# Condensing channel statistics as the last measuring step, and exchanging which engine copies which convolution outcome, in the first layer of a four-layer network

## The chip, the core and the metric

The kernel runs on one core of one Trainium2 chip. A core has a matrix engine (TensorE, "PE" in the profile; its weight loads are listed apart as "PEld"), VectorE ("DVE"), ScalarE ("ACT"), GpSimd ("POOL") and SyncE ("SP"), which issues most of the DMA. Every engine works through its own list of instructions in order and waits for the others by semaphores. The metric is the device time of one execution in microseconds (us), lower is better; the time of a kernel is the median of its runs.

## What is computed

The input is a batch of 8 images of 56x56 pixels with 192 channels, float32. Four layers follow each other, each of the form `x = x + layer(groupnorm(x))`. The change lies in layer 0 and in the statistics that layer 0 leaves for layer 1. Cut to what matters:

```python
def _gn(v, G=32, eps=1e-5):          # 32 groups of 6 channels, per image
    g = v.reshape(B, H, W, 32, 6)
    m, s = g.mean((1, 2, 4)), g.var((1, 2, 4))
    return (g - m) / sqrt(s + eps)

def layer0(x):                       # x: normalized, 8 x 56 x 56 x 192
    p, q, v = silu(x @ Wp + bp), silu(x @ Wq + bq), silu(x @ Wv + bv)   # 576 channels each
    qv = q * v
    o1 = toeplitz(qv along width, a1)    # per channel, a 56x56 Toeplitz matrix
    o2 = toeplitz(qv along height, a2)
    return (p * (o1 + o2)) @ Wo + bo
x = x + layer0(_gn(x)); x = x + layer1(_gn(x)); x = x + layer2(_gn(x)); x = x + layer3(_gn(x))
```

## The kernel before

**Tiling.** Layer 0 takes one image `b` after another. The 576 channels of `q*v` are cut into 9 subchunks of 64 channels; they are worked on in five blocks `c` = 0 to 4 of two subchunks each (the last block has one). A block consists of these steps:

- `project`: for each of four groups of pixel rows, `gate` multiplies by the weights (12 matmuls, line 356) and ScalarE takes silu of the result into a buffer `s` (L364); `products` then multiplies q by v: `straight` on VectorE (L378), `across` on GpSimd and partly on VectorE (L384). All of them write the tile `qv`.
- `turn_both` (or `turn` in the last block): seven (four) steps in which TensorE transposes a part of `qv` into PSUM (L411, L430); VectorE copies one half of it out (tile `ol`) and after it ScalarE the other (tile `or`), L416 and L437.
- `convolve`: for each of its subchunks two steps q = 0 and 1 of 32 matmuls (L454). Each step fills one PSUM tile, its "outcome", which one engine copies into the tile `ot`: VectorE for q = 0 (L474), ScalarE for q = 1 (L472). A block has so four such steps, and four copies, one after the other. In the last block (`tail`) the two engines share each copy in another way (L465), which the change leaves alone.
- After the blocks 1 and 3, `post` works off a pair of blocks: `gate` (12 matmuls a part, L496, silu in L503), `back` (transposes of `ot`, L515, and a multiplication, L520), `out` and `rest` (L529, L550) with sums into the image's result `acca`, `accb` (L481, L483). `post_tail` does so after block 4.

**PSUM.** `banks()` hands out PSUM tiles in a ring: three tiles named `c`, and every fourth time one named `o` (in the blocks 2 and 4 the `o` tile is used by `out`, and `banks()` gives `c` alone while the steps of `post` run). A matmul that wants a tile waits until the copies out of its last content are done. The buffers `s` are a ring of six.

**Statistics.** `gn.steps` returns for a set of spans a list of measuring steps (`measure`, one `bn_stats` each, L156), and two more functions. `deviate` condenses the measured statistics with one `bn_aggr` for each span (L160), copies the means into one tile (L161), and hands them to `spread`, which multiplies them by a small matrix on TensorE (L129) and copies the result back (L137, L138); then come three small VectorE operations (L163, L164, L165). `settle` spreads the deviations (L129 again), takes the root on ScalarE (L170) and forms scale and bias (L171, L172). There are two users:

- `normalize(nxt)`, the next image's input, measured in block 2 (12 measuring steps);
- `tell(b - 1, ...)`, the finished image's result, for layer 1 (11 measuring steps: six in block 0, the other five in block 1). Its `deviate` and `last` are the list `telling`. For the last image, `tell` is called after the loop: its steps run at the end of layer 0, and its `telling` goes to `cx.late`, which layer 1 calls.

**Order.** The order of the instructions of TensorE, VectorE and ScalarE is the program's own (`manual_schedule`). In block 1 it is

```python
merge(weave(fill, [f for fs, _ in early for f in fs]), turns, measures)
for _, f in early: f()                      # products of the groups 0 and 1
...
beside = [lambda f=f: f(banks) for f in telling]
ahead = whole(ahead, beside)                # groups 2 and 3: gates, one of beside, products
```

`weave` spreads several lists evenly over one another, so that the seven turns, the gates of the first groups and the measuring steps alternate. `whole` puts `deviate` between the gates of group 2 and its products, and `last` between the gates of group 3 and its products. After that come the four convolution steps. In block 3 the products of the last group stand in front of the first convolution step, and `post` follows the fourth. The transfers on SyncE and GpSimd's work are put in order by a scheduler.

Of the kernel before, what the change touches and what calls it, by code (L numbers as in the profile page):

```python
# [99 lines left out]
class GroupNormSplit:  # L100
# [40 lines left out]
    def steps(self, *spans):  # L141

        cx, nc = self.cx, self.cx.nc
        c = len(spans)
        new = lambda name: cx.tile(self.small, [128, c], f"{name}{c}")
        mv = cx.tile(self.small, [128, c, 2], f"mv{c}")
        mean, dev, told = new("mean"), new("dev"), {}
        parts = [  # L150
            (x, n, cx.tile(self.small, [128, n, 6], f"st{c}{k}")) for k, (x, n) in enumerate(spans)
        ]

        def measure(x, n, st, j):
            w = x.shape[-1] // n
            nc.vector.bn_stats(st[:, j, :], x[:, j * w : (j + 1) * w])  # L156

        def deviate(bank):
            for k, (_, _, st) in enumerate(parts):
                nc.vector.bn_aggr(mv[:, k, :], st.rearrange("p a b -> p (a b)"))  # L160
            nc.vector.tensor_copy(mean, mv[:, :, 0])  # L161
            told["gms"] = gms = self.spread(bank, mean)
            nc.vector.tensor_tensor(dev, mean, gms, ALU.subtract)  # L163
            nc.vector.tensor_tensor(dev, dev, dev, ALU.mult)  # L164
            nc.vector.tensor_tensor(dev, dev, mv[:, :, 1], ALU.add)  # L165

        def settle(bank):
            sd, rstd, nbias = new("sd"), new("rstd"), new("nbias")
            gms = told["gms"]
            nc.scalar.activation(sd, self.spread(bank, dev), AF.Sqrt, bias=self.eps)  # L170
            nc.vector.reciprocal(rstd, sd)  # L171
            nc.vector.scalar_tensor_tensor(nbias, gms, -1.0, rstd, ALU.mult, ALU.mult)  # L172
            return rstd, nbias

        return [lambda p=p, j=j: measure(*p, j) for p in parts for j in range(p[1])], deviate, settle


def layer0(cx, xin, xout, w, consts):
# [6 lines left out]
    tc, nc = cx.tc, cx.nc  # L185
# [8 lines left out]
    with ExitStack() as es:  # L194
# [9 lines left out]
        def banks():  # L204
            if ring["wide"]:
                ring["at"] += 1
                if ring["at"] % 4 == 0:
                    return cx.tile(psc, [128, 2, 512], "o", bufs=1)
            return cx.tile(psc, [128, 2, 512], "c")
# [231 lines left out]
        def convolve(n, ot):  # L441


            s = n % NS
            left, right = pairs[n % 2]
            tail = s == NS - 1

            def step(q):
                ps = banks()
                for k in range(2):  # L450
                    for v in range(8):
                        for u in range(2):
                            d = q * 16 + 8 * k + v + u * 32
                            nc.tensor.matmul(  # L454
                                ps[u * 64 : (u + 1) * 64, k, v * H : (v + 1) * H],
                                left[:, d * H : d * H + 64],
                                right[:, d * H : (d + 1) * H],
                                start=True, stop=True, skip_group_check=True,
                            )
                if tail:  # L460
                    for u, copy in enumerate((nc.vector.tensor_copy, nc.scalar.copy)):
                        d0 = q * 16 + u * 32
                        dst = ot[0:H, :, d0 : d0 + 16].rearrange("p h (k v) -> p h k v", k=2)
                        src = ps[u * 64 : u * 64 + H, :, 0 : 8 * H]
                        copy(dst, src.rearrange("p k (v h) -> p h k v", h=H))  # L465
                    return
                else:
                    d0 = s % 4 * 32 + 16 * q
                    dst = ot[:, :, d0 : d0 + 16].rearrange("p h (k v) -> p h k v", k=2)
                    src = ps[0:120, :, 0 : 8 * H].rearrange("p k (v h) -> p h k v", h=H)  # L470
                if q % 2:
                    nc.scalar.copy(dst, src)  # L472
                else:
                    nc.vector.tensor_copy(dst, src)  # L474

            return [lambda q=q: step(q) for q in range(2)]

        def add(m, j, x, ps):
# [114 lines left out]
        def post_tail(xn, ot, acc):  # L593
# [67 lines left out]

            steps = [lambda f=f, g=g: f(g) for f in (gate, back, out) for g in range(2)]
            return [*steps, lambda: (rest(0), rest(1))]

        def ready(v):
# [3 lines left out]
        def normalize(xn):  # L669

            measures, deviate, settle = gn.steps(*((xn[:, k], 4) for k in range(3)))

            def last():
                rstd, nbias = settle(banks)
                ready(rstd)
                for k in (0, 2):
                    affine(nc.vector, xn[:, k], xn[:, k], rstd[:, k : k + 1], nbias[:, k : k + 1])
                nc.scalar.activation(
                    xn[:, 1], xn[:, 1], AF.Identity, bias=nbias[:, 1:2], scale=rstd[:, 1:2]
                )  # L680

            return measures, [lambda: deviate(banks), last]

        def tell(b, xa, xb):

            measures, deviate, settle = gn.steps((xa, 7), (xb, 4))

            def last(bank):
                nn = cx.tile(gn.small, [128, 2, 2], "nn")
                told = settle(bank)  # L690
                if b + 1 < B:
                    ready(told[0])
                for i, v in enumerate(told):
                    nc.vector.tensor_copy(nn[:, :, i], v)
                nc.sync.dma_start(cx.norms[b][0:CA], nn[:, 0, :])
                nc.sync.dma_start(cx.norms[b][CA:], nn[0:CB, 1, :])

            return measures, [deviate, last]
# [25 lines left out]
        def whole(steps, beside=()):  # L724

            k, n = len(beside), max(len(steps), 1)
            cuts = [beside[-(-i * k // n) : -(-(i + 1) * k // n)] for i in range(n)]
            return [
                lambda fs=fs, h=h, cut=cut: [f() for f in (*fs, *cut, h)]
                for (fs, h), cut in zip(steps, cuts)  # L730
            ]

        merge(whole(project(xn, 0)))
        fill, after, telling, measures = [], None, [], []
        for b in range(B):
            more = b + 1 < B
            for c in range(NC):
# [9 lines left out]
                if c == 2 and more:  # L747
                    measures, normalizing = normalize(nxt)
                merge(weave(fill, [f for fs, _ in early for f in fs]), turns, measures)
                measures = []  # L750
# [8 lines left out]
                if c == 0:  # L759
                    if after is not None:  # L760
                        image_dma(nc.sync, xout[b - 1], *after, store=True)
                        measures, telling = tell(b - 1, *after)
                        beside, measures = measures[:6], measures[6:]
# [1475 lines left out]
```

## Time and profile before

The kernel's median was 4032.93 us in 3 runs (4031.6 to 4044.12). The profiled execution took 4030.25 us by itself, 2.68 us less than the median; its span from the first to the last instruction is 4028.5 us, so 1.75 us lie around it.

| stretch of the profiled execution | us | TensorE busy | VectorE busy | ScalarE busy | GpSimd busy |
|---|---|---|---|---|---|
| whole span | 4028.5 | 3786.9 | 2382.0 | 1792.8 | 1511.3 |
| 640 to 880, a piece of layer 0 | 240 | 229.25 | 149.77 | 107.18 | 75.27 |
| 880 to 1120, a piece of layer 0 | 240 | 229.43 | 153.35 | 110.30 | 75.43 |
| 2160 to 4028, the layers after | 1868 | 1782.96 | 1089.68 | 874.30 | 837.36 |

Layer 0 ends shortly after 1890 us. One image takes about 229 us there: the stretch in which the means of the finished image are spread starts at 578.96, 807.98, 1036.21 and so on.

How to read the lines further down. A line of the waits reads: engine, tile and line that waited, what it waited for, the time in total, how often, the longest. A line of the timeline has the start, the duration (of the whole group when several are merged, xcount), engine, line, operation, output and input with shapes, and in brackets the idle time of that engine just before and what ended it. A line of the windows has the stretch, its length, the busy time, then the clock that TensorE was granted (1.00 is full speed), the share of the DMA engines and GB/s.

### The profile page before, as it was taken

Reading aid. Unit: us, or ns where it says so; the run is one execution under the profiler, and the core shown is the slowest. Engines: PE = TensorE matmul, PEld = TensorE weight load, DVE = VectorE, ACT = ScalarE, POOL = GpSimd, SP = SyncE. Lnnn points to the kernel's source line nnn. Section 1 sums busy time; section 2 is a strip of 40 time slices with the busy share of each in tenths; the row PEclk is TensorE's granted clock in tenths of the full one; section 3 lists DMA queues with packets and bytes.
Section 4 is the critical chain, followed back from the end, with each engine's and each line's share of the span. In section 5 each row is a group of like instructions: output and inputs, shape, how many; then the busy total and the mean of one; then the engine's idle time right before and its main releaser. Section 6 shows DMA issues by size and latency. Waiting matters only on the chain.

```text
span 4028.5 us, 115826 instructions
## 1 busy us (share of the span) xinstructions
PE 3786.9 (94%) x51036; PEld 2655.0 (66%) x51036; DVE 2382.0 (59%) x3270; ACT 1792.8 (45%) x2036; POOL 1511.3 (38%) x1325
## 2 busy tenths in 40 slices
PE   6989999999999999998899999899989999998997
PEld 4777767777777767776566666444445455556997
DVE  5647666665656666556444444666666667665664
ACT  2444444443444444343343343244345555554663
POOL 3222242323232242223333333333334444444776
PEclk9999999999999999999899999999999999999999
DMA  7865262434426253333344443556557766653333
GB/s 158 168 139 146 78 169 78 129 85 111 103 82 165 78 141 94 88 93 106 77 109 104 113 95 96 173 174 198 176 162 187 178 147 153 152 139 102 99 101 99
DMA packets 390300, 507.94 MB, mean 126 GB/s; under 512 B 176932, under 2 KB 326724, under 8 KB 388404
## 3 DMA queue, kind: packets, MB, share of 16 engines
q1 hardware_dynamic: 385621, 494.07, 47.3%
q8 instruction: 401, 6.57, 0.7%
q10 hardware_dynamic: 3135, 3.47, 0.3%
q0 software_dynamic: 1040, 2.99, 0.3%
q14 instruction: 103, 0.84, 0.1%
HBM read 344.69 MB, written 155.65 MB: 124 GB/s over the span
## 4 chain that ended last, share of the span: by engine, by line
PE 73%; DVE 9%; issue 6%; DMA 4%; ACT 3%; POOL 2%; SPq 1%; DVEq 0%; POOLq 0%; ACTq 0%
PE c L356 9%; PE h L2072 8%; PE v L1560 6%; PE c L496 5%; PE c L454 4%; PE o L529 4%; PE c L1079 4%; PE o L356 3%; PE y L1114 3%; PE kv L1620 3%; PE c L550 2%; PE c L1085 2%; DVE qv L378 2%; PE c L1782 2%; DVE ol L416 2%
## 5 line engine op out<-in xcount | busy, mean ns | idle before, releaser
L384 POOL TENSOR_TENSOR qv<-s,s 128x392 f32<-128x392 f32 (+3 forms) x320 | 556.6, 1767 | 1274.6 <-ACT s L364 881.3
L356 PE MATMUL c<-x,wqv 64*128 64x392 f32 x2592 | 474.9, 511 | 12.4 <-ACT s L364 9.4
L356 PEld LDWEIGHTS c<-x,wqv 64*128 64x128 f32 x2592 | 253.9, 194 | 171.8 <-issue 14.2
L364 ACT ACTIVATE s<-c,bqv 128x784 f32<-128x784 f32 (+1 forms) x247 | 224.8, 913 | 245.0 <-PE c L356 188.2
L496 PE MATMUL c<-x,wp 64*128 64x224 f32 x2688 | 284.7, 357 | 22.5 <-DVE ot L474 12.4
L378 DVE TENSOR_TENSOR qv<-s,s 128x784 f32<-128x784 f32 (+1 forms) x160 | 241.2, 1523 | 98.5 <-ACT s L364 98.5
L416 DVE COPY ol<-c 56x1024 f32<-56x1024 f32 x184 | 221.1, 1210 | 102.7 <-PE c L411 102.7
L416 ACT COPY or<-c 56x1024 f32<-56x1024 f32 x184 | 183.8, 1008 | 219.1 <-DVE ol L416 218.2
L496 PEld LDWEIGHTS c<-x,wp 64*128 64x128 f32 x2688 | 256.2, 190 | 27.5 <-DVE ot L474 13.2
L520 DVE TENSOR_TENSOR s<-s,c 128x896 f32<-128x896 f32 x112 | 121.8, 1088 | 254.5 <-ACT s L503 242.4
L454 PEld LDWEIGHTS c<-or,ol 120*64 120x64 f32 x7168 | 216.0, 139 | 20.3 <-issue 15.2
L454 PE MATMUL c<-or,ol 120*64 120x56 f32 x7168 | 222.5, 223 | 5.1 <-ACT or L416 2.4
L1571 ACT ACTIVATE vb<-sm 128x1024 f32<-128x1024 f32 (+1 forms) x100 | 103.9, 1040 | 262.6 <-issue 218.1
L503 ACT ACTIVATE s<-c,bp 128x448 f32<-128x448 f32 x224 | 129.9, 631 | 204.1 <-PE c L496 201.5
L2103 POOL TENSOR_TENSOR y<-y,s 128x448 f32<-128x448 f32 x168 | 185.0, 1101 | 88.8 <-ACT s L2082 88.8
L2072 PE MATMUL h<-ringv,am 128*64 128x57 f32 (+1 forms) x4400 | 191.4, 234 | 17.5 <-DVE ringv L2059 10.6
L1560 PE MATMUL v<-wvb,wa 128*128 128x512 f32 (+1 forms) x400 | 192.1, 613 | 6.1 <-ACT wa L1446 6.1
L2072 PE MATMUL h<-ringh,am 128*64 128x57 f32 (+1 forms) x4400 | 186.3, 231 | 7.8 <-DVE ringh L2078 7.8
L2072 PEld LDWEIGHTS h<-ringv,am 128*64 128x64 f32 x4400 | 167.1, 139 | 20.8 <-DVE ringv L2059 11.5
L1079 PE MATMUL c<-wv,xc 128*126 128x192 f32 x896 | 175.4, 339 | 0.0
L2072 PEld LDWEIGHTS h<-ringh,am 128*64 128x64 f32 x4400 | 166.2, 139 | 10.0 <-DVE ringh L2078 9.9
L1589 POOL TENSOR_TENSOR l<-vb,ta 128x512 f32<-128x512 f32 (+1 forms) x52 | 75.2, 1446 | 259.4 <-ACT vb L1571 258.5
(269 smaller groups left out, 7819.9 us busy)
## 6 DMA issues: line engine op xcount, KB each, us to landing
or<-tt SPq DMA_DIRECT2D x252, 196.0 KB
ol<-tt SPq DMA_DIRECT2D x252, 196.0 KB
vt<-v SPq DMA_DIRECT2D x56, 672.0 KB
v<-vb SPq DMA_DIRECT2D x96, 384.0 KB
x<-x SPq DMA_DIRECT2D x110, 168.0 KB
wqv<-in_l_w_qv SPq DMA_DIRECT2D x38, 384.0 KB
x<-in_x SPq DMA_DIRECT2D x64, 196.0 KB
x<-x SPq DMA_DIRECT2D x110, 112.0 KB
```

What stands on the lines that cost most here:

```text
L356: nc.tensor.matmul(ps[:, h, 0:n], wqv[q][rows, k, i, :], xn[rows, k, g * n : (g + 1) * n], start=(k == 0), stop=(k == 2),)
L364: nc.scalar.activation(t, ps[rows, :, 0:n], AF.Silu, bias=bqv[rows, j : j + 1])
L378: nc.vector.tensor_tensor(sub(qv[rows, 7 * g :, 64 + H - 1 :], (HH * 120, 2), (120, 7), (-1, H)), *(t.rearrange("p u (h w) -> p u h w", w= ...
L384: eng.tensor_tensor(sub(qv[rows, w0:, H - 1 - 7 * g - HH * u :], (120, w1 - w0), (-1, 7)), *(t[:, u].rearrange("p (h w) -> p w h", w=H)[:, ...
L416: copy(dst[:, :, :, i0 : i0 + 8], view[rows])
L454: nc.tensor.matmul(ps[u * 64 : (u + 1) * 64, k, v * H : (v + 1) * H], left[:, d * H : d * H + 64], right[:, d * H : (d + 1) * H], start=Tr ...
L496: nc.tensor.matmul(ps[:, h, u * n : (u + 1) * n], wps[j][rows, k, u, :], xn[rows, k, g * n : (g + 1) * n], start=(u == 0 and k == 0), stop ...
L529: nc.tensor.matmul(outs[q][:, h, i * n : (i + 1) * n], wo[rows, 2 * j + u, 0:CA], gated[g][rows, u, h * n : (h + 1) * n], start=(i == 0 an ...
L1079: nc.tensor.matmul(out(i, u), group(i, u), wv[0], start=(u == 0), stop=True, skip_group_check=True,)
L1560: nc.tensor.matmul(out, x[:, at : at + n], wt, start=(k == 0), stop=(k == 1), skip_group_check=True,)
L2072: nc.tensor.matmul(ps[sides[c], y], am[a][:, m * CB : (m + 1) * CB], old[:, x], start=(n < 2), stop=True, skip_group_check=True,)
L2103: nc.gpsimd.tensor_tensor(v, v, line[:, j], ALU.add)
```

## The change

The two `bn_aggr` or three, and the copy of the means, are taken out of `deviate` into a function `average`, which becomes one more step at the end of the list of measuring steps. And in `convolve` the two engines are exchanged: ScalarE copies the outcome of q = 0, VectorE that of q = 1.

```diff
-        def deviate(bank):
+        def average():
             for k, (_, _, st) in enumerate(parts):
                 nc.vector.bn_aggr(mv[:, k, :], st.rearrange("p a b -> p (a b)"))
             nc.vector.tensor_copy(mean, mv[:, :, 0])
+
+        def deviate(bank):
             told["gms"] = gms = self.spread(bank, mean)
...
-        return [lambda p=p, j=j: measure(*p, j) for p in parts for j in range(p[1])], deviate, settle
+        measures = [lambda p=p, j=j: measure(*p, j) for p in parts for j in range(p[1])]
+        return [*measures, average], deviate, settle
...
                 if q % 2:
+                    nc.vector.tensor_copy(dst, src)
+                else:
                     nc.scalar.copy(dst, src)
-                else:
-                    nc.vector.tensor_copy(dst, src)
```

The lists of `normalize` and `tell` get so 13 and 12 measuring steps. In the built program TensorE's and GpSimd's instructions stand in the same order as before. On VectorE, in block 1 of the images 1 to 7, the three instructions of `average` (L160 twice, L161) move from behind the two products of the groups 0 and 1 to a place in front of the last turn's copy (L416); the five measurements there move up by up to one turn. In block 2 `average` stays where it was and single measurements change places with a neighbouring copy. At the end of layer 0 the three instructions move from layer 1 to right behind the last measurement. On SyncE, three loads of `accb` (line 73, in block 1 of each image but the first) move in between those of `acca`; no transfer is added or removed.

## The prediction

> **What bounds the kernel now.** First the page, its busy times and the chain that ended last:
>
> ```profile
> PE 3786.9 (94%) x51036; PEld 2655.0 (66%) x51036; DVE 2382.0 (59%) x3270; ACT 1792.8 (45%) x2036; POOL 1511.3 (38%) x1325
> ...
> PE 73%; DVE 9%; issue 6%; DMA 4%; ACT 3%; POOL 2%; SPq 1%; DVEq 0%; POOLq 0%; ACTq 0%
> ```
>
> TensorE is busy 94% and carries 73% of the chain. The change touches VectorE and ScalarE alone, so it is worth only what TensorE waits for them: next, the waits of TensorE.
>
> ```profile
> PE c L129 <- DVE mean L161: 22.7, 7, 3.2
> ...
> PE c L496 <- DVE ot L474: 12.4, 6, 2.5
> ...
> PE b L129 <- DVE mean L161: 4.1, 1, 4.1
> ```
>
> The first row is seven waits of some 3.24 us, one in block 1 of the images 1 to 7 (counted from 0). The second is six, one in block 3 of the images 1 to 6. The third is one, in layer 1. Now the timeline of block 1 of image 2, all engines:
>
> ```profile
> 571.29 1.22 DVE L416 COPY ol<-c 56x1024 f32<-56x1024 f32 x1 [0.65 <-PE c L411]
> ...
> 571.90 11.50 POOL L384 TENSOR_TENSOR qv<-s,s 128x392 f32<-128x392 f32 x6 [15.83 <-PE c L411]
> ...
> 572.91 1.20 DVE L416 COPY ol<-c 56x1024 f32<-56x1024 f32 x1
> ...
> 573.59 2.14 PE L356 MATMUL o<-x,wqv 64*128 64x392 f32 x12
> 574.03 3.33 DVE L378 TENSOR_TENSOR qv<-s,s 128x784 f32<-128x784 f32 x2
> ...
> 577.29 0.45 DVE L160 BATCH_NORM_AGGREGATE mv<-st 128x2 f32<-128x42 f32 x2
> 577.78 1.04 DVE L161 COPY mean<-mv 128x2 f32<-128x2 f32 x1
> ...
> 578.96 1.06 PE L129 MATMUL c<-mean,gmat 64*128 64x1 f32 x16 [3.24 <-DVE mean L161]
> ...
> 579.85 5.92 PE L356 MATMUL c<-x,wqv 64*128 64x392 f32 x24
> ...
> 580.45 1.43 DVE L163 TENSOR_TENSOR dev<-mean,spread 128x2 f32<-128x2 f32 x1
> ...
> 585.58 0.98 PE L129 MATMUL o<-dev,gmat 64*128 64x1 f32 x16
> ```
>
> TensorE has the last gate of group 2 done at 575.73 and wants the means. VectorE condenses them at 577.29, because the products of groups 0 and 1 (574.03, 3.33 us) stand in front; and the copy of the means takes 1.04 us beside GpSimd (it is 0.17 us at 1983.11, with GpSimd idle). Then 24 matmuls take 5.92 us where 36 take 5.92 us elsewhere. The clock windows say why:
>
> ```profile
> 579.00:583.00 4.00, 4.00 (x28) 0.68 0.03 9
> 583.00:586.00 3.00, 3.00 (x24) 0.86 0.00 0
> ```
>
> The loss, 4 x 0.32 + 3 x 0.14 = 1.70 us, is half clock for 3.41 us. In windows of 1 us such an event follows each of the seven waits. Block 3, image 2, then the same place in image 7, where the ring of PSUM tiles is one step further on:
>
> ```profile
> 685.35 1.90 DVE L384 TENSOR_TENSOR qv<-s,s 64x196 f32<-64x196 f32 x1
> ...
> 687.17 1.07 DVE L474 COPY ot<-c 120x896 f32<-120x896 f32 x1
> ...
> 688.18 1.07 DVE L474 COPY ot<-o 120x896 f32<-120x896 f32 x1
> ...
> 688.30 3.59 PE L496 MATMUL c<-x,wp 64*128 64x224 f32 x24 [2.55 <-DVE ot L474]
> ...
> 691.68 1.05 PE L515 MATMUL c<-ident,ot 56*128 56x56 f32 x16
> ```
>
> ```profile
> 1834.82 2.54 PE L496 MATMUL c<-x,wp 64*128 64x224 f32 x24
> ...
> 1838.55 0.70 PE L515 MATMUL c<-ident,ot 56*128 56x56 f32 x16 [1.19 <-DVE ot L474]
> ```
>
> In image 2 the gate of `post` (688.30) wants the PSUM tile that held the first convolution outcome, and VectorE, still in the products of block 3 (to 687.2), has not copied it. In image 7 the gate (1834.82) gets a tile without waiting, and only `back` (L515) waits, 1.19 us, for VectorE's second copy.
>
> **Block 1, the mean.** What moves is two L160 (0.45 us together) and one L161; no DMA is in it. `average` now stands between the sixth and the seventh turn's copy, at 572.43. The measurement that stood there moves a turn up, into VectorE's idle 0.65 us before 571.29; the one before it pushes the fifth turn's copy back by some 0.5 us, of which ScalarE, copying two turns in a row, passes 0.15 us to TensorE. GpSimd starts its products at 571.90, so I charge L161 its 1.04 us and not 0.17: means at 573.9. The last turn's copy goes from 572.91 to 573.9, the two products to 575.0 to 578.3, ScalarE's copy of that turn ends at 576.1 instead of 575.15. TensorE: last gate of group 2 to 575.9, spread to 576.95 without wait, then the gates of group 3, whose tiles come free at 576.1 and 577.0 (silu of group 2, 0.9 us later than before): 576.9 to 581.0 at full clock. What is late next is the second spread: VectorE does the spread's copies at 578.3, L163 and L164 beside GpSimd (1.43 and 1.50 us as before), L165: 581.7. TensorE waits 0.7 us, spreads, and starts the convolution at 582.7 instead of 586.5. Its tiles are free: the silu of group 3 ends at 579.9 and 582.0 by then. The four steps take 7.6 us, to 590.25 instead of 594.10. `post` begins there: its tile was ScalarE's copy (queued behind root and table loads, done at 586.7), and `back` at 592.4 needs VectorE's last copy, 590.4 to 591.5. So 3.85 us an image, x 7 = 27.0 us. Bounds: 4.95 us (wait 3.24 and clock 1.71, no second wait) gives 34.6; if each of the three operations is held 1.04 us, `average` costs 3.1 instead of 1.5, all after it comes 1.6 us later, 2.2 us are left, and that gives 15.6.
>
> The Trainium skill, "TensorE: Matmul & The Clock Gate" (Part 1), states that the clock halves after at least one idle window of about 3.4 us. Here it halves after idle times of 3.24 us, and of 1.18 us at 447.22; the length of the slow phase, 3.41 us, agrees. By that rule the loss would not hang on these waits, and the sum would be that of the second rival below.
>
> **The copies.** Eight copies of 1.08 us (L474) and eight of 0.91 us (L472) an image stay as many; the four of a block went to VectorE, ScalarE, VectorE, ScalarE in turn, and now begin with ScalarE. In blocks 0 and 2 the last copy is now VectorE's; its next work, a turn's copy, comes 2.9 us after the convolution ends (idle 2.88 us at 438.09), which covers 1.08 us; uncovered it were up to 1.08 us a block. In block 3 ScalarE has its last silu done when the first step ends (682.06 in image 2), so the gate's tile is free about 4 us early and the gate starts when the convolution ends. VectorE's two copies stand behind the products as before, so `back` still waits for the second: the picture of image 7. There the next gate (L496) starts at 1839.90, 1.35 us after `back`. Image 2: the second copy ends at 689.25, `back` starts at 689.35, the next gate at 690.7 instead of 693.60: 2.9 us, of which up to 1.71 us are clock. Image 1, whose wait was 1.60 us and cost no clock: `back` 461.4, next gate 462.75 instead of 464.21, 1.45 us. Three images are of each kind: 3 x 1.45 + 3 x 2.9 = 13.1 us; if the remaining idle of 1.2 to 1.4 us still halves the clock in the three, 8.0. Idle of 1.17 to 1.19 us did so in three images (447, 904, 1597) and not in four, so I take 10.
>
> **The rest.** In layer 1 the wait of 4.10 us ends by the means being old; but VectorE takes the spread's copy up only behind three L142-type measurements that end at 1982.7, so the second spread ends at 1985.3 instead of 1987.96: 2.65 us (0 if layer 1's loads are late next). `average` itself lies in VectorE's idle 2.48 us before 1901.02. In block 2 the order around TensorE's waits is the same, and moved measurements (0.55 us) lie in idle of 2 us and more before L520: nothing. SyncE's reordered loads are needed some 35 us later: nothing.
>
> Sum: 27.0 + 10 + 2.65 = 39.6 us. Profiled execution 4030.25 - 39.6 = 3990.6; the median lies 2.68 us above, so 3993.3.
>
> **Rivals.** *VectorE hands back part* (0.14): `average` is held at each operation; 15.6 + 2.65 + 10 = 28.2, so 4005. For it: L163 and L164 are held each time. Against: L160 took 0.45 us for two beside GpSimd.
> *The clock does not follow the waits* (0.12): group 3 still loses 1.71 us an image; 3.85 becomes 2.14, x 7 = 15, the copies give 8: 25.7, so 4007. Against it: seven events after seven waits.
> *The change does not do what it says* (0.06): what releases TensorE at 578.96 is another thing that the profile puts down to L161; then only the copies and the clock in part, 10 us, 4023. Against: the matmul starts 0.14 us after the copy of the means ends, each time.
> *Slower* (0.04): GpSimd's hold on VectorE. If all six small operations (`average`, L163 to L165) pay the longest hold found on such an operation, 2.01 us (L1318), `average` costs 6.0 instead of 1.5 and the other three 6.0 instead of 3.1: 7.4 us more, minus the 3.85 won, 3.6 us later an image, 25 us; less 12.65 from the rest, 12.5 us slower, 4045. It decides from 5.7 us of extra hold an image. Against: L163 to L165 show 3.1 us in nearly every image.
> The Trainium skill, "SBUF — State Buffer" (Who interferes with whom), speaks on this side: a VectorE copy from SBUF and GpSimd exclude each other for a whole instruction. L161's 1.04 us beside GpSimd against 0.17 agrees.
>
> **How the numbers follow.** The forecast has 0.64. The forecast's own bounds are 34.6 + 13.1 + 2.65 = 50 us (3983) and the first two rivals' 4007; with a few us for the clock's phase the range is 3979 to 4011, which leaves out the last two rivals and some of the forecast. About 0.3% (12 us) is what a measurement of this kernel can tell: faster 0.64 + 0.14 + 0.12 = 0.90, same 0.06, slower 0.04.
>
> **What would show it.** Right: no wait of L129 on L161; L129 on L165 some 0.7 us in its place; granted clock 1.00 in the gates of group 3; the gate L496 without wait for L474 and L515 waiting 1 to 1.4 us for VectorE; images 223 us apart instead of 229. Wrong: a wait on L161 that remains, group 3 at half clock, or the convolution of block 1 or L515 of block 2 waiting for VectorE.

## The result and the profile after

The changed kernel takes 4018.61 us (median of 10 runs, 4011.09 to 4030.38) against 4033.03 us of the kernel before on the same chip: a ratio of 0.9966, 95% interval 0.9953 to 0.9978. It is faster, by 14.4 us, where 39.6 were forecast. The profiled execution took 4015.87 us, its span 4014.1, which is also 14.4 us below the one before.

The page of the kernel after, busy times and the chain that ended last:

```profile
PE 3783.2 (94%) x51036; PEld 2655.3 (66%) x51036; DVE 2398.0 (60%) x3270; ACT 1792.6 (45%) x2036; POOL 1518.4 (38%) x1325
...
PE 69%; DVE 9%; issue 8%; DMA 4%; ACT 3%; POOL 3%; SPq 3%; ACTq 0%; POOLq 0%; DVEq 0%
```

VectorE is 16 us busier (2398.0 against 2382.0), with the same number of instructions. Lines of the changed kernel are two or three higher than before (L163 to L165 are now L165 to L167, L496 is L499, L515 is L518, L454 is L457; L160 and L161 keep their numbers). TensorE's waits (engine, tile, line, what it waited for; total, times, longest):

```profile
PE o L129 <- DVE dev L167: 19.5, 7, 3.1
...
PE c L518 <- DVE ot L475: 6.0, 6, 1.2
...
PE b L129 <- DVE x L1182: 1.9, 1, 1.9
PE c L499 <- DVE ot L475: 1.6, 1, 1.6
```

The seven waits for the means (22.7 us) are gone, and seven for the deviations stand in their place: 19.5 us, so 2.8 each. The six waits of `post`'s gate (12.4 us) have become six shorter ones of `back` (6.0). The VectorE groups of layer 0 in the kernel after (shapes kept apart; busy us, then the mean ns of one) say what grew:

```profile
L166 DVE TENSOR_TENSOR dev<-dev 128x2 f32<-128x2 f32 x7 | 10.5, 1497 | 0.2
L167 DVE TENSOR_TENSOR dev<-dev,mv 128x2 f32<-128x2 f32 x7 | 10.4, 1488 | 0.2
...
L165 DVE TENSOR_TENSOR dev<-mean,spread 128x2 f32<-128x2 f32 x7 | 8.3, 1180 | 0.2
```

and the same in the kernel before (L163, L164 and L165 there):

```profile
L164 DVE TENSOR_TENSOR dev<-dev 128x2 f32<-128x2 f32 x7 | 10.5, 1499 | 0.2
...
L163 DVE TENSOR_TENSOR dev<-mean,spread 128x2 f32<-128x2 f32 x7 | 9.2, 1313 | 0.2
...
L165 DVE TENSOR_TENSOR dev<-dev,mv 128x2 f32<-128x2 f32 x7 | 1.1, 161 | 0.2
```

Adding the variances took 0.16 us seven times and now takes 1.49 us seven times. The timeline of block 1 of image 2 shows why; first VectorE, then GpSimd (two short stretches, two instructions in each row), then TensorE:

```profile
579.86 0.45 DVE L160 BATCH_NORM_AGGREGATE mv<-st 128x2 f32<-128x42 f32 x2
580.34 0.61 DVE L161 COPY mean<-mv 128x2 f32<-128x2 f32 x1
580.87 1.21 DVE L419 COPY ol<-c 56x1024 f32<-56x1024 f32 x1
582.00 4.40 DVE L381 TENSOR_TENSOR qv<-s,s 128x784 f32<-128x784 f32 x2
...
586.51 0.16 DVE L138 TENSOR_TENSOR spread<-c,spread 128x2 f32<-128x2 f32 x1
586.70 1.18 DVE L165 TENSOR_TENSOR dev<-mean,spread 128x2 f32<-128x2 f32 x1
587.92 1.50 DVE L166 TENSOR_TENSOR dev<-dev 128x2 f32<-128x2 f32 x1
589.45 1.49 DVE L167 TENSOR_TENSOR dev<-dev,mv 128x2 f32<-128x2 f32 x1
```

```profile
585.53 3.87 POOL L387 TENSOR_TENSOR qv<-s,s 128x392 f32<-128x392 f32 x2
```

```profile
587.83 3.09 POOL L387 TENSOR_TENSOR qv<-s,s 128x392 f32<-128x392 f32 x2
```

```profile
584.02 4.20 PE L359 MATMUL c<-x,wqv 64*128 64x392 f32 x24
591.08 1.06 PE L129 MATMUL o<-dev,gmat 64*128 64x1 f32 x16 [2.86 <-DVE dev L167]
592.07 7.36 PE L457 MATMUL c<-or,ol 120*64 120x56 f32 x192
```

GpSimd's instructions change at 587.83, 589.40 and 590.92; the three small operations end at 587.88, 589.42 and 590.94. Each ends with a GpSimd instruction. The addition just before them (L138, 586.51) is also a 128x2 operation of two tensors, but reads one of them from PSUM; it runs in the middle of a GpSimd instruction and takes 0.16 us.

The copy of the means (L161) reads only one tensor, and it too ends with a GpSimd instruction. GpSimd's first one:

```profile
579.33 1.60 POOL L387 TENSOR_TENSOR qv<-s,s 128x392 f32<-128x392 f32 x1 [15.76 <-PE c L414]
```

It ends at 579.33 + 1.60 = 580.93, the copy at 580.34 + 0.61 = 580.95. In the kernel before the copy ended at 577.78 + 1.04 = 578.82 and GpSimd's third instruction at 578.79, in image 2; in all seven images of either kernel it ends 0.02 to 0.03 us after a GpSimd instruction. So `average` is cheap here (0.45 and 0.61 us) because a GpSimd instruction happens to end soon. The gates of group 3 run at full clock (4.20 us instead of 5.92), and then TensorE stands 2.86 us for the deviations. The windows of TensorE behind that wait (stretch, length, busy, granted clock):

```profile
584.00:588.00 4.00, 4.00 (x28) 1.00 0.79 187
588.00:592.00 4.00, 1.14 (x18) 1.00 0.33 98
592.00:595.00 3.00, 3.00 (x69) 0.64 0.02 5
595.00:598.00 3.00, 3.00 (x90) 0.80 0.64 84
```

3 x 0.36 + 3 x 0.20 = 1.68 us are lost: the event of half clock has moved from the gates to the convolution, whose first 192 matmuls take 7.36 us (5.81 in the kernel before, where no wait precedes them). In the seven images they take 7.18 to 7.97 us.

For the experiments, one table. It cuts the period of an image by four of TensorE's instructions: the first matmul of `post_tail`'s gate, the spread of the finished image's means, the spread of its deviations, and the spread of the next image's means in block 2. Means over the images 1 to 6 (1 to 7 for the second and third stretch), from the starts in each timeline; the last column is 1 minus the granted clock, summed over windows of 1 us from 100 us to the last image's `post_tail`. Each row is one execution, and the chips differ (the kernel before took 4033 us beside the kernel after and 4043 to 4048 us in the groups below; the execution in its row took 4030), so a difference of some tenths of a us between two rows says little.

| kernel | block 2 (means) to tail, us | tail to means | means to deviations | deviations to block 2 | period | clock lost in layer 0 |
|---|---|---|---|---|---|---|
| before | 109.0 | 58.2 | 6.8 | 56.1 | 230.0 | 32.4 |
| after | 106.5 | 55.0 | 7.8 | 58.5 | 227.7 | 30.7 |
| e1 condensing only | 108.9 | 55.3 | 7.8 | 58.9 | 230.9 | 30.7 |
| e2 exchange only | 106.6 | 58.2 | 7.9 | 56.4 | 229.1 | 37.5 |
| e3 after + columns | 106.6 | 55.0 | 4.8 | 55.5 | 222.0 | 15.4 |
| e4 deviations among the turns | 106.6 | 48.5 | 8.6 | 63.3 | 226.8 | 20.5 |
| e5 after again | 106.5 | 55.0 | 7.9 | 58.5 | 227.9 | 32.4 |
| e6 before + columns | 108.9 | 58.3 | 7.0 | 55.9 | 230.2 | 34.1 |
| e7 exchange + columns | 106.5 | 58.3 | 7.8 | 56.6 | 229.2 | 32.4 |
| e8 condensing + columns | 108.8 | 55.0 | 4.8 | 55.3 | 223.9 | 20.5 |
| e9 two held | 106.6 | 55.0 | 6.5 | 56.6 | 224.8 | 23.9 |
| e10 four held | 106.5 | 55.1 | 8.6 | 59.0 | 229.2 | 34.1 |
| e11 less GpSimd | 106.6 | 55.0 | 5.2 | 56.9 | 223.6 | 17.1 |
| e12 e3 + copies on ScalarE | 106.4 | 55.0 | 4.8 | 55.3 | 221.6 | 11.9 |

Read "before" against "after": the exchange of the copies is in the first column (2.4 us an image), the condensing in the second (3.2 us), and the third and fourth give all of the second back (1.0 + 2.4). The six periods make 13.9 of the 14.4 us between the two spans; the first image (4.5 us longer), the last period (1.7 longer) and the later layers (6.8 shorter) nearly cancel.

### The profile page after: what moved, and what is told of

It reads as the page before. It is cut to its first block, busy times and chain, and to the rows that moved or that the text cites. A ratio compares the mean times of both kernels' runs of the same rounds, so it can differ in the third digit from the quotient of the medians.

```text
span 4014.1 us, 115826 instructions
## 1 busy us (share of the span) xinstructions
PE 3783.2 (94%) x51036; PEld 2655.3 (66%) x51036; DVE 2398.0 (60%) x3270; ACT 1792.6 (45%) x2036; POOL 1518.4 (38%) x1325
## 4 chain that ended last, share of the span: by engine, by line
PE 69%; DVE 9%; issue 8%; DMA 4%; ACT 3%; POOL 3%; SPq 3%; ACTq 0%; POOLq 0%; DVEq 0%
PE c L359 9%; PE v L1563 6%; PE h L2075 6%; PE c L499 5%; PE c L457 4%; PE o L532 4%; PE c L1082 4%; PE o L359 3%; PE y L1117 3%; PE kv L1623 3%; PE c L553 2%; DVE qv L381 2%; PE c L1088 2%; DVE ol L419 2%; PE c L1785 1%
## 5 line engine op out<-in xcount | busy, mean ns | idle before, releaser
L359 PE MATMUL c<-x,wqv 64*128 64x392 f32 x2592 | 461.3, 500 | 12.4 <-ACT s L367 9.4
L359 PEld LDWEIGHTS c<-x,wqv 64*128 64x128 f32 x2592 | 245.0, 189 | 167.4 <-ACT s L367 10.5
L367 ACT ACTIVATE s<-c,bqv 128x784 f32<-128x784 f32 (+1 forms) x247 | 224.6, 912 | 221.6 <-PE c L359 213.4
L381 DVE TENSOR_TENSOR qv<-s,s 128x784 f32<-128x784 f32 (+1 forms) x160 | 249.6, 1575 | 99.5 <-ACT s L367 99.5
L499 PE MATMUL c<-x,wp 64*128 64x224 f32 x2688 | 282.3, 355 | 13.8 <-issue 5.6
L419 DVE COPY ol<-c 56x1024 f32<-56x1024 f32 x184 | 221.6, 1210 | 88.5 <-PE c L414 88.5
L499 PEld LDWEIGHTS c<-x,wp 64*128 64x128 f32 x2688 | 254.7, 188 | 17.7 <-ACT s L506 7.5
L457 PEld LDWEIGHTS c<-or,ol 120*64 120x64 f32 x7168 | 229.0, 145 | 23.0 <-issue 15.4
L457 PE MATMUL c<-or,ol 120*64 120x56 f32 x7168 | 235.4, 230 | 8.0 <-DMA ol<-ed 4.1
```

What stands on the lines that cost most here:

```text
L359: nc.tensor.matmul(ps[:, h, 0:n], wqv[q][rows, k, i, :], xn[rows, k, g * n : (g + 1) * n], start=(k == 0), stop=(k == 2),)
L367: nc.scalar.activation(t, ps[rows, :, 0:n], AF.Silu, bias=bqv[rows, j : j + 1])
L381: nc.vector.tensor_tensor(sub(qv[rows, 7 * g :, 64 + H - 1 :], (HH * 120, 2), (120, 7), (-1, H)), *(t.rearrange("p u (h w) -> p u h w", w= ...
L419: copy(dst[:, :, :, i0 : i0 + 8], view[rows])
L457: nc.tensor.matmul(ps[u * 64 : (u + 1) * 64, k, v * H : (v + 1) * H], left[:, d * H : d * H + 64], right[:, d * H : (d + 1) * H], start=Tr ...
L499: nc.tensor.matmul(ps[:, h, u * n : (u + 1) * n], wps[j][rows, k, u, :], xn[rows, k, g * n : (g + 1) * n], start=(u == 0 and k == 0), stop ...
```

## The experiments

The theory: a small VectorE operation with two input tensors in SBUF can't end before the GpSimd instruction that runs beside it, so it costs one GpSimd instruction, whatever its size; the change took away the pause of GpSimd in which the third one had run free. The rivals: the operations are slow by their form or VectorE's queue; the clock loses the time whatever waits; the exchange of the copies loses what the condensing wins. Each group of four kernels ran on one chip of its own, and each ratio is to the kernel before on that chip (medians there 4048.19, 4046.14 and 4042.5 us). A ratio is followed by its 95% interval.

### First group: the halves, and two ways round the hold

**e1, the condensing alone.** The copies go back to their engines.

```diff
-                    nc.vector.tensor_copy(dst, src)
-                else:
                     nc.scalar.copy(dst, src)
+                else:
+                    nc.vector.tensor_copy(dst, src)
```

> The changed kernel with the copies of the convolution outcomes given back to the engines of before; only the condensing is moved. Theory (the stall moved): the wait on L161 is gone, but the three small VectorE operations L165 to L167 each wait for a GpSimd instruction to end, so TensorE waits some 2.9 us in the second spread and the half clock falls on the convolution instead of on the gates: no gain, 4033 within 5 us, and the six waits for L475 of 1.6 to 2.5 us in block 3 are there again. Rival (the condensing gave the 14 us and the copies nothing): 4019. The recorded forecast would have had 4003 here.

Measured: 4042.14 us, ratio 0.9984 (0.9971 to 0.9996). TensorE's waits:

```profile
PE o L129 <- DVE dev L167: 19.4, 7, 3.1
...
PE c L499 <- DVE ot L477: 14.2, 6, 2.5
```

The wait for the deviations comes with the condensing. By itself the condensing, forecast at 27 us, is worth 6. Where these 6 us lie isn't shown: in the one execution profiled, an image takes 230.9 us, no less than before.

**e2, the exchange alone.** The kernel before with the copies exchanged; the condensing stays in `deviate`.

```diff
                 if q % 2:
+                    nc.vector.tensor_copy(dst, src)
+                else:
                     nc.scalar.copy(dst, src)
-                else:
-                    nc.vector.tensor_copy(dst, src)
```

> The kernel before with the copies alone exchanged. Theory: all of the gain is here: block 2's first spread to the tail's first gate becomes 106.4 us instead of 108.2 to 109.8 in the images 1 to 6, about 14 us, so 4019 within 4 us; the seven waits on L161 of 3.24 us and the half clock behind them stay. Rival (the condensing gave the gain): 4033.

Measured: 4040.9 us, ratio 0.998 (0.997 to 0.999). Block 3 gains the whole of what it gains in the kernel after (table, first column: 2.4 us an image, 14 us in six), but only 7 us arrive. In this profile 5.1 us more clock is lost in layer 0 than before. Block 1 of image 2 shows where:

```profile
579.76 1.78 PE L129 MATMUL c<-mean,gmat 64*128 64x1 f32 x16 [3.25 <-DVE mean L161]
581.34 6.88 PE L356 MATMUL c<-x,wqv 64*128 64x392 f32 x24
```

The wait is the old one, 3.25 us, yet spread and gates take 1.78 and 6.88 us where they took 1.06 and 5.92: the half clock covers more of them. That is so in six of the seven images here, and in one of seven in the kernel before. Which stretch of the clock a wait costs depends on something that moved with the shorter block 3; what, these runs don't say. The halves add up to about the whole: 6.0 + 7.3 = 13.3 us, against 14.4.

**e3, the change with the small operations column by column.** Each operation handles one column and takes its second operand as one scalar per partition, not as a second tensor.

```diff
-            nc.vector.tensor_tensor(dev, mean, gms, ALU.subtract)
-            nc.vector.tensor_tensor(dev, dev, dev, ALU.mult)
-            nc.vector.tensor_tensor(dev, dev, mv[:, :, 1], ALU.add)
+            for k in range(c):
+                one = slice(k, k + 1)
+                nc.vector.tensor_scalar(dev[:, one], mean[:, one], gms[:, one], None, ALU.subtract)
+            for k in range(c):
+                one = slice(k, k + 1)
+                nc.vector.tensor_scalar(
+                    dev[:, one], dev[:, one], dev[:, one], mv[:, k, 1:2], ALU.mult, ALU.add
+                )
```

> The changed kernel, with L165 to L167 written column by column with the other operands as scalars for each partition (two operations a column: subtract; multiply and add), so that no operation reads two tensors. Theory: the hold is that of operations with two tensors beside GpSimd; the new ones take some 0.2 us each, the second spread's wait falls from 2.86 us to under 0.7, no half clock behind it: 2.2 to 4.5 us an image less, 4003 to 3987. Rival (VectorE's backlog from the condensing and the longer products, not the small operations, makes the second spread late): the wait stays above 2 us and the time at 4019 within 5.

Measured: 3990.35 us, ratio 0.986 (0.9842 to 0.9878). Image 2, VectorE and then TensorE:

```profile
576.83 0.33 DVE L167 TENSOR_SCALAR dev<-mean,spread 128x1 f32<-128x1 f32 x2
577.08 0.46 DVE L170 TENSOR_SCALAR dev<-dev,mv 128x1 f32<-128x1 f32 x2
```

```profile
578.99 0.95 PE L129 MATMUL o<-dev,gmat 64*128 64x1 f32 x16
579.87 5.81 PE L462 MATMUL c<-or,ol 120*64 120x56 f32 x192
```

Four instructions take some 0.7 us, beside a GpSimd that runs without pause from 570.25, where three took 4.2. No wait is left in either spread, the convolution has the full clock, and the period falls to 222.0 us. The clock rival falls with it: half of the loss in layer 0 goes with the waits (30.7 to 15.4 us).

**e4, the deviations moved in front of GpSimd.** The measurements are taken two at a time, the condensing follows the third turn, and `deviate` the fifth.

```diff
+                if c == 1 and measures:
+                    a, b0, c0, d0, e0, mean_of = measures
+                    measures = [
+                        lambda: (a(), b0()), lambda: (c0(), d0()), lambda: (e0(), mean_of()),
+                        lambda: telling.pop(0)(banks), lambda: None,
+                    ]
```

> The changed kernel, where in block 1 the five measurements stand two by two behind the first turns, the condensing behind the third, and the whole of deviate (first spread and small operations) behind the fifth, before GpSimd has work. Theory: small operations of 0.16 us, no wait in either spread, no half clock: 4.5 us an image less than the changed kernel, 3987, or up to 3995 if the measurements push the turns' copies by 1 us. Rival (VectorE's backlog): the turns become late and the time stays at 4019 or rises.

Measured: 4020.74 us, ratio 0.9939 (0.9922 to 0.9955). The untouched operations are short here, because GpSimd has not begun (it starts at 574.87 in image 2):

```profile
573.01 0.16 DVE L165 TENSOR_TENSOR dev<-mean,spread 128x2 f32<-128x2 f32 x1
573.20 0.16 DVE L166 TENSOR_TENSOR dev<-dev 128x2 f32<-128x2 f32 x1
573.40 0.16 DVE L167 TENSOR_TENSOR dev<-dev,mv 128x2 f32<-128x2 f32 x1
```

So the form is not slow by itself. The copy of the means, at 570.30, takes 0.17 us here. But more than half of e3's gain is missing: means to block 2 takes 8.6 + 63.3 us, 11.6 more than in e3, of which 6.6 only answer to the earlier means; TensorE waits 1.1 us for the means, and idle time for which the profile shows no cause ("issue") is 1.5 to 4.4 us an image, where the kernel after has 0 to 3.7. That idle time is unexplained.

### Second group: with and without the hold

Here the columns are combined with each half, and the changed kernel is run again.

**e5, the changed kernel again.** No edit.

> The changed kernel once more, beside the kernel before on the same chip, and as the foot of the three kernels that follow. In the first profiles the first image took 4.5 us longer with the change (a DMA wait of the convolution, 4.09 instead of 2.21 us, and clock), and the layers after layer 0 6.8 us less. Theory 'drift': both are of that one execution; here the block-2 means of the first image come at 175 +- 2 us and the rest after layer 0's last tail takes as long as in the kernels with one half of the change (2155 to 2156 us); ratio 0.995 to 0.998. Theory 'part of the change': first image again at 179 us or more, and the rest some 7 us below that.

Measured: 4029.33 us, ratio 0.996 (0.9945 to 0.9975), as at first. In the first pair of profiles, block 2 of the first image had its means 4.5 us later with the change (179.5 against 175.0 us). It is 179.7 here, but 179.0 in e6, which has neither half of the change, and 175.1 in e4, which has both. The layers after layer 0 take 2152.9 us here, 2141.4 in the first profile of the same kernel. Both differences of the first pair of profiles are scatter of single executions, not the change.

**e6, e7, e8: the edit of e3 in the kernel before, in e2 and in e1.**

> The kernel before, without either half of the change, but with the three small operations behind the spread written column by column (mean minus spread, square, plus variance, with the second operand as a scalar for each partition). Theory 'hold': these operations were held, one for each GpSimd instruction, but in the kernel before TensorE waits for the means and not for them (no wait of L129 on the deviations), so freeing them is worth nothing: ratio 0.997 to 1.003, seven waits of some 3.2 us on the means as before, and small operations of 0.15 to 0.25 us. Rival 'columns pay by themselves': the 44 us that they brought on top of the change (4035 to 3990) come here too, ratio 0.987 to 0.992.

Measured: 4045.73 us, ratio 0.9995 (0.9983 to 1.0007).

> The exchange of the copies with the small operations column by column; the condensing stays where it was. Theory 'hold': as the exchange alone (0.998), since the waits on the means stay: 0.995 to 1.000. Rival 'columns pay by themselves': 0.985 to 0.990.

Measured: 4034.27 us, ratio 0.9973 (0.996 to 0.9986).

> The condensing as the last step of measuring, with the small operations column by column; the copies stay with their engines. Theory 'hold': this is the pair that does the work. Neither spread waits; means to deviations 4.8 us and the full-clock convolution save 4 to 6 us an image, 28 to 42 us in all: ratio 0.9895 to 0.993. Together with the exchange (which was worth up to 14 us in block 3) this makes the 0.986 measured. Rival: the copies matter here, and without their exchange the gain is lost again in block 3: ratio above 0.995.

Measured: 4002.8 us, ratio 0.9888 (0.9871 to 0.9905), a little more than the forecast range.

TensorE's waits of e6 (first) keep the two old rows; of those two e8 (second) has only that of `post`'s gate for VectorE's copy, and its waits hold no row for either spread of the images 1 to 7:

```profile
PE c L129 <- DVE mean L161: 22.7, 7, 3.3
...
PE c L501 <- DVE ot L479: 11.7, 6, 2.5
```

```profile
PE c L504 <- DVE ot L482: 11.9, 6, 2.5
```

The columns are worth nothing where TensorE waits for the means (e6), nothing that can be told on top of the exchange (e7 against e2), and everything on top of the condensing: 0.9984 becomes 0.9888. The condensing, worth 6 us with the hold, is worth 43 without it (4046.14 - 4002.8). The hold lay in the kernel before as well, 1.31 and 1.50 us in two of the three operations. These two cost nothing there, since TensorE's wait for the means came first and left the gates of group 3 to cover them. The hold on the copy of the means (1.04 us instead of 0.17) stood right in front of that wait, so an estimated 0.9 of its 3.2 us was this hold too; e6 doesn't touch that copy, and no run shows what it is worth.

### Third group: how much one operation costs, and who holds it

**e9 and e10: two held operations, and four, instead of three.** e9 writes only the last one by columns; e10 adds a maximum that leaves the value as it is.

```diff
 # e9
-            nc.vector.tensor_tensor(dev, dev, mv[:, :, 1], ALU.add)
+            for k in range(c):
+                one = slice(k, k + 1)
+                nc.vector.tensor_scalar(dev[:, one], dev[:, one], mv[:, k, 1:2], None, ALU.add)
 # e10
             nc.vector.tensor_tensor(dev, dev, mv[:, :, 1], ALU.add)
+            nc.vector.tensor_tensor(dev, dev, mv[:, :, 1], ALU.max)
```

> The changed kernel with only the last of the three small operations (plus variance) written column by column; the first two take two tensors as before. Theory 'one GpSimd instruction for each operation of two tensors': the first two end with a GpSimd instruction each (about 1.2 and 1.5 us), the last takes some 0.35 us for both columns; the wait of the second spread (L129) falls by 1.1 to 1.2 us, from 2.86 to about 1.7, means to deviations from 7.9 to 6.7 us; 8 us in all or somewhat more if the clock recovers: ratio 0.990 to 0.9955. Rival 'the hold is one for the group, whatever its length' (VectorE waits once until GpSimd is through): wait unchanged at 2.8 us, ratio 0.996.

Measured: 4012.02 us, ratio 0.992 (0.990 to 0.994). Image 2:

```profile
582.02 1.06 PE L129 MATMUL o<-dev,gmat 64*128 64x1 f32 x16 [1.58 <-DVE dev L169]
583.01 5.81 PE L459 MATMUL c<-or,ol 120*64 120x56 f32 x192
```

> The changed kernel with a fourth small operation of two tensors behind the three (the maximum of the sum and the variance, which leaves the value as it is). Theory 'one GpSimd instruction for each operation of two tensors': GpSimd still has instructions queued there, so the fourth takes 1.5 us; the wait of the second spread rises from 2.86 to about 4.4 us, means to deviations from 7.9 to 9.4 us, 10 us in all and perhaps some clock: ratio 0.998 to 1.002. Rival 'the hold is one for the group': 0.16 us more an image, ratio 0.996.

Measured: 4032.64 us, ratio 0.9981 (0.9971 to 0.9992). Image 2, VectorE, GpSimd's seventh instruction, TensorE:

```profile
589.30 1.49 DVE L167 TENSOR_TENSOR dev<-dev,mv 128x2 f32<-128x2 f32 x1
590.83 0.79 DVE L168 TENSOR_TENSOR dev<-dev,mv 128x2 f32<-128x2 f32 x1
```

```profile
590.73 0.88 POOL L388 TENSOR_TENSOR qv<-s,s 128x196 f32<-128x196 f32 x1
```

```profile
591.76 1.87 PE L129 MATMUL o<-dev,gmat 64*128 64x1 f32 x16 [3.67 <-DVE dev L168]
593.56 7.99 PE L458 MATMUL c<-or,ol 120*64 120x56 f32 x192
```

The wait follows the count: 1.5 us with two, 2.8 with three, 3.6 with four. The fourth step was forecast at 1.5 us and was 0.8, because the GpSimd instruction that runs by then is one of half the size: it ends at 590.73 + 0.88 = 591.61, the held operation at 591.62. So the price is that of GpSimd's instruction, not one of VectorE's. In image 2 of e9 the wait of 1.58 us leaves the convolution at full clock, where 2.86 us do not. It is not always so; image 6 of e9:

```profile
1479.18 1.31 PE L129 MATMUL o<-dev,gmat 64*128 64x1 f32 x16 [1.60 <-DVE dev L169]
1480.42 8.62 PE L459 MATMUL c<-or,ol 120*64 120x56 f32 x192
```

The 192 matmuls take 5.81 us in four of e9's seven images and 7.36, 7.36 and 8.62 in three, where the kernel after is slow in all seven. So one operation less saves its 1.3 us and, in some images, the half clock behind it.

**e11, less work for GpSimd.** The operations stay as they are; the kernel leaves out GpSimd's products of group 2 in block 1 (`without` is true there alone).

```diff
-                for u in range(2):
+                for u in [] if without else range(2):
                     across(nc.gpsimd, u, 0, H)
```

> The changed kernel, without GpSimd's two products of group 2 in block 1 (the part of q times v along the width of those pixel rows is left out there). GpSimd is then through its first four instructions when the three small operations come. Theory 'GpSimd's instructions hold them': they take some 0.16 us each, the second spread does not wait, means to deviations 4.8 us and the convolution at full clock, although they are still operations of two tensors: ratio 0.983 to 0.989, as with the columns. Rival 'it is the form of the operation, or VectorE's own queue, that is slow there': 1.2 to 1.5 us each as before, ratio 0.996.

Measured: 3994.3 us, ratio 0.9878 (0.9859 to 0.9896). Image 2:

```profile
584.61 1.18 DVE L165 TENSOR_TENSOR dev<-mean,spread 128x2 f32<-128x2 f32 x1
585.82 0.16 DVE L166 TENSOR_TENSOR dev<-dev 128x2 f32<-128x2 f32 x1
586.02 0.16 DVE L167 TENSOR_TENSOR dev<-dev,mv 128x2 f32<-128x2 f32 x1
```

```profile
577.22 8.55 POOL L387 TENSOR_TENSOR qv<-s,s 128x392 f32<-128x392 f32 x4 [15.80 <-PE c L414]
```

GpSimd's last instruction ends at 585.77, the first small operation at 585.79, and the other two take 0.16 us each. It is GpSimd that holds them: same form, same queue, same place.

Which operations are held can be read from the rows of the kernel after. Beside GpSimd, those of two SBUF tensors are (L165 to L167), and so is the copy of the means from SBUF to SBUF; L138, with one of its tensors in PSUM, and the reciprocal of one 128x2 tensor (L173, 0.16 to 0.17 us) are not. The column operations differ from the held ones in two ways, one column instead of two and a scalar instead of a tensor; no run separates these.

**e12, a better version.** e3, with all four copies of block 3 on ScalarE.

```diff
-                if q % 2:
+                if q % 2 and s not in (6, 7):
                     nc.vector.tensor_copy(dst, src)
```

> An attempt at a better version: the change with the column-wise small operations, and in block 3 all four copies of the convolution's outcomes on ScalarE (in the other blocks ScalarE and VectorE in turn, as in the change). If the transposes of post (back) wait there only for VectorE's second copy behind its products, six waits of 0.7 us go: 4 us below the columns with the change, ratio 0.984 to 0.9865. Rival: ScalarE becomes late instead, its fourth copy holds up the silu of post's gate, and the ratio is 0.986 or above.

Measured: 3974.09 us, ratio 0.9831 (0.9817 to 0.9846), below both kernels; it is also below e3's 0.986 (0.9842 to 0.9878), on another chip and with intervals that overlap a little. No wait of `back` for `ot` is left (e3 still had 4.2 us in six). The first column of the table falls by only 0.2 us an image, though; of the 19.7 us between the two spans, 3.2 lie in the first image, 4.3 in the last period and 8.9 in the layers that the edit doesn't touch, so how much of it belongs to the edit is not settled.

## Why the prediction was right or wrong

**The removed wait: right.** No wait for the means remains, `average` costs 1.06 us (1.5 were charged), the gates of group 3 run at full clock (4.20 us; the prediction's comparison, 36 matmuls in 5.92 us, is 6.09 in the rows), and the first spread starts 3.2 us earlier behind the tail.

**The second spread: this step failed.** The prediction took the two held operations at 1.43 and 1.50 us "as before" and L165 at 0.16, and came to a wait of 0.7 us. Those durations are not VectorE's. Each is the time to the end of a GpSimd instruction (L163 to 581.88, L164 to 583.41, GpSimd's fifth and sixth to 581.86 and 583.40), and the 0.16 of L165 belonged to a GpSimd that had finished its first six then and stood idle, because TensorE's own wait kept group 3 back. Take that wait away, and GpSimd runs its eight without a gap: the third operation is held too (1.49), and the two products in front of them, both now beside GpSimd, take 4.40 us instead of 3.33. Add 1.3 and 1.1 us for these two, and take off 0.4 since the copy of the means took 0.61 us and not 1.04, and 0.7 becomes 2.7; 2.86 were measured. That it took 0.61 was luck: how far the next end of a GpSimd instruction was when it started. e3, e8, e9, e10 and e11 show the hold on the small operations from five sides; the 1.1 us of the products is read from the rows alone.

**The clock: the mechanism right, its consequence missed.** The event was to vanish with the wait. It followed the new wait instead (1.68 us on the convolution). For block 1 of image 2 the sum is so -3.24 - 1.72 (gates) + 2.86 + 1.55 (convolution) = -0.55 us, not -3.85. Over the images even that is gone: tail to block 2 is 121.1 us before and 121.2 after. Some of the rest is idle time without a shown cause, 3.71 us once behind block 1 of image 1; the kernel before has such time too, up to 2.25 us in an image, and its cause stays open.

**The copies: right, the term somewhat small.** The pictures predicted for `back` came (1.16 us in image 2, in place of the gate's 2.55). The six stretches from block 2 to the tail are 14.6 us shorter; 10 were taken, 13.1 was the upper end. In e2 half of it is lost again to the clock, in a place that the exchange doesn't touch, and e7 has the same longer stretch there (7.8 us from the means to the deviations, 6.8 before). Why a wait costs sometimes no clock, sometimes 1.7 us and sometimes 3.4 is what these runs leave unexplained.

**Layer 1:** its wait of 4.10 us fell to 1.9, now for a measurement; the 2.65 us forecast can't be told from the scatter of the later layers (2141 to 2162 us in all these profiles).

**The rivals.** The slower case named the right mechanism, GpSimd's hold on the small operations, but priced it by a longest hold on all six and gave it 0.04; the case "VectorE hands back part" put the hold on each operation of `average`, where only the copy was held, by 0.44 us. Neither asked what GpSimd would be doing at the new time. By its number the third rival (4023 us) came nearest, by accident: its reason, that another thing than the copy of the means releases TensorE, is refuted by the waits that went. The second rival had group 3 still at half clock; its gates took 4.20 us in all seven images. The Trainium skill, "SBUF — State Buffer" (Who interferes with whom), says that a VectorE instruction with two SBUF inputs contends with a GpSimd instruction that reads SBUF; e10 and e11 agree, with 0.79 to 1.50 us each beside GpSimd and 0.16 without.

## What to carry to other kernels

A duration that one engine's row shows may be another engine's: before moving a short instruction, see what ends with it, and take its price from what the other engine will be doing at the new time, above all when the wait that is to go is what gave that engine its pause. Where GpSimd runs beside them, write small VectorE operations on a critical path so that they don't take two SBUF tensors (here one column and a scalar per partition): that made a gain of 6 us one of 43. And look at small copies within SBUF, which were held here too. And follow a removed stall to the next join; here the stall and its half clock came back one spread later almost whole.

## What the hardware showed that was not expected

- In block 1 of the changed kernel a 128x2 operation of two SBUF tensors took 1.18 to 1.50 us beside GpSimd's products of 1.6 to 2.3 us and in e10 0.79 us beside one of 0.88, ending within 0.05 us of the GpSimd instruction each time; two column operations took 0.33 to 0.46 us in the same place.
- The 128x2 copy of the means within SBUF was held in the same way: 1.04 us before, 0.61 after, 0.17 without GpSimd (e4).
- TensorE at half clock followed all seven idle times of 2.05 to 3.14 us in front of the second spread of the kernel after, and three of e9's seven of 1.07 to 1.60 us at the same place; in the kernel before it also followed one of 1.18 us at 447.22, and not one of 1.60 us at 460.37. So the length of a single idle time doesn't decide it alone.
